# The last image of a two-layer network: bilinear corners gathered from one table per tap instead of one table for all taps

## The chip, the cores and the metric

The kernel runs on one core of a Trainium2 chip. The metric is the device time of one execution in microseconds (us), the median of three runs. The engines are named as in the profile: PE is TensorE (matrix products), DVE is VectorE, ACT is ScalarE, POOL is GpSimd, SP is the engine that issues most DMAs. Each engine works through its own list of instructions in order.

## The reference, cut to what matters

Eight images of 128 channels and 32 by 32 points pass through two layers. The first layer is an attention over columns and rows followed by a long causal convolution (the "spectral" part). The second layer is a deformable convolution with three taps followed by a mixture of eight experts. The change touches only the second layer, and mostly the deformable convolution:

```python
for j in range(K):                                   # K = 3 taps
    y  = h_grid + offset[:, 2 * j]
    xc = w_base + j + offset[:, 2 * j + 1]
    ...
    samp = gather(iy0, ix0) * (1 - wy) * (1 - wx) + gather(iy0, ix0 + 1) * (1 - wy) * wx \
         + gather(iy0 + 1, ix0) * wy * (1 - wx) + gather(iy0 + 1, ix0 + 1) * wy * wx
    samp = samp * mask[:, j][..., None]
    out = out + jnp.einsum('bhwc,oc->bohw', samp, conv_w[:, :, 0, j])
```

For every point and every tap, four corners are read, each is multiplied by a weight, and the twelve products are added up. After that come a normalisation over the channels, a choice of two experts out of eight per point, and the weighted sum of their outputs.

## The kernel before, in words

**Order of the whole.** A first part (up to about 920 us) computes the attention. Then one long loop, `spectral_and_second_layer`, runs over 8 images times 16 filters. Each step issues the spectral products of its filter, and after each small group of them it calls `advance`, which hands out a fixed amount of "time" to two rows of side work. Side work is the second layer of the image before, written as generators that `yield` their own price. The amount handed out is `RATE` (3.2) for images 0 to 6 and `LAST_RATE` (3.6) while the last image, number 7, passes through the spectral part. The program's order on every engine is exactly the order in which these generators issue; nothing reorders it later. When the spectral part of image 7 is done, its own second layer (`layer.image`, which calls `points` and then `sampled` with `alone=True`) is interleaved, step by step, with what is left of image 6's second layer.

**points.** `turn_back` transposes the result back to 128 points x 8 blocks x 128 channels and adds the residual (`tok`, line 1182). `norm_steps` (lines 788 to 795) normalises it. `turn_steps` transposes it. Then, for each of eight blocks of 128 points, one product `p_g` (line 1037) makes the three tap images (3 x 128 values per point) and 27 more values; ScalarE copies the block to `gs` (line 1040). Since the convolution's weights are applied first, a corner is a row of a tap image. `write` (line 1030) stores each tap image four times, shifted by 0, 1, 32 and 33 rows, so that one row of the DRAM table `tab` holds the four corners of a point side by side (4 x 128 numbers, 2 KB). That makes 3 taps x 4 slots x 2 halves = 24 DMAs of 256 KB each. For the last image the slots alternate between SP's queue and ScalarE's queue. `corners` (lines 950 to 981) computes the row numbers `cn_idx` and the weights `w`; between the two, ScalarE makes the exponential of the mask (line 972).

**sampled.** GpSimd issues one indirect DMA (line 1089) per block of points and tap, 24 in all; each fetches 128 rows of 2 KB into one third of a tile `g` (three tiles in rotation). For the last image ScalarE multiplies the corners of taps 0 and 1 by their weights (line 1107, eight instructions per block), VectorE those of tap 2 in one instruction (line 1111), adds all twelve in one reduction (line 1115) and adds `tok` (line 1118). Then follow the normalisation, the gates (lines 1191 to 1228) and, for each block, the experts: two products `p_e` (line 1135), four scalings by ScalarE (line 1142), a product, a reduction and an addition by VectorE (lines 1147, 1152, 1155). After each half of the blocks, `p_out` (lines 1164 and 1167) transposes the result, ScalarE copies it to `ot` (line 1170), and after both halves one DMA of 512 KB writes the image out (line 1172).

**What an instruction waits for.** The waits are placed per DRAM tile: a gather waits until every earlier write to the table it reads has landed. Before the change one table per image parity holds all three taps.

Of the kernel before, what the change touches and what calls it, by code (L numbers as in the profile page):

```python
# [11 lines left out]
F32 = mybir.dt.float32  # L12
I32 = mybir.dt.int32
# [21 lines left out]
RATE = 3.2  # L35
LAST_RATE = 3.6

# [765 lines left out]
class DeformAndExperts:  # L803
# [17 lines left out]
    def setup(self):  # L821
# [30 lines left out]
        for g in range(4):  # L852
# [6 lines left out]
        self.row = cp.tile([P, NT, TAPS], F32, name="row")  # L859
        nc.gpsimd.iota(self.row, pattern=[[0, NT], [self.ROWS, TAPS]], base=33,  # L860
                       channel_multiplier=0, allow_small_or_imprecise_dtypes=True)
# [4 lines left out]
        for n in range(2):  # L866
            tab = dram.tile([TAPS, self.ROWS, 4, C], F32, name=f"tab{n}")
            for tap in range(TAPS):
                for r0 in (0, T):
                    nc.sync.dma_start(  # L870
                        tab[tap, r0 : r0 + 33].rearrange("r s c -> r (s c)"), zero
                    )
                yield
            self.tabs.append(tab)
# [128 lines left out]
    def points(self, b, x2, got, alone, x1):  # L1003
# [21 lines left out]
        def write():  # L1025
            if writes:
                i0, tap, slot, back = writes.pop(0)
                r0 = 33 - back + i0 * P
                queue = nc.scalar if alone and slot % 2 else nc.sync
                queue.dma_start(  # L1030
                    tab[tap, r0 : r0 + 4 * P, slot, :].rearrange("(i p) c -> p i c", p=P),
                    gs[:, i0 : i0 + 4, tap * C : (tap + 1) * C],
                )

        for i in range(NT):
# [5 lines left out]
            if i % 4 == 3:  # L1041
                writes += [
                    (i - 3, tap, slot, back)
                    for tap in range(TAPS) for slot, back in enumerate((0, 1, 32, 33))
                ]
            for _ in range(4 if alone else 2):
                write()
# [20 lines left out]
    def sampled(self, b, got, alone):  # L1068
# [6 lines left out]
        x3 = sb.tile([P, NT, C], F32, tag="x3", name="x3")  # L1075
        rows = self.tabs[b % 2].rearrange("t r s c -> (t r) (s c)")
        points = [(i, tap) for i in range(NT) for tap in range(TAPS)]
        fetched, here, tiles = [], [], []

        def fetch():  # L1080
            if len(fetched) < len(points):
                i, tap = points[len(fetched)]
                if tap == 0:
                    tiles.append(sb.tile([P, TAPS, 4, C], F32, tag="g", name="g", bufs=3))
                    if not alone:
                        here.append(sb.tile([P, TAPS], I32, tag="here", name="here", bufs=3))
                        nc.scalar.copy(here[-1], idx[:, i, :])
                at = idx[:, i, tap : tap + 1] if alone else here[-1][:, tap : tap + 1]
                nc.gpsimd.indirect_dma_start(  # L1089
                    out=tiles[-1][:, tap].rearrange("p k c -> p (k c)"), out_offset=None, in_=rows,  # L1090
                    in_offset=bass.IndirectOffsetOnAxis(ap=at, axis=0),
                )
                fetched.append((i, tap))

        if not alone:
            yield 8.0
        for _ in range(4):
            fetch()
            yield 1.0 if alone else 2.6
        for _ in range(2 if alone else 5):  # L1100
            yield
        for i, tap in points:
# [7 lines left out]
            else:  # L1110
# [7 lines left out]
                nc.vector.tensor_add(x3[:, i, :], x3[:, i, :], tok[:, i, :])  # L1118
            yield 1.7 if alone else 2.6
        tt = sb.tile([P, NT, C], F32, tag="ht", name="tt")  # L1120
# [9 lines left out]
        for i in range(NT):  # L1130
# [26 lines left out]
            if i % 4 == 3:  # L1157
# [4 lines left out]
                for k in range(4):  # L1162
# [6 lines left out]
                    )  # L1169
                nc.scalar.copy(ot[:, half * 512 : half * 512 + 512], po)  # L1170
                yield
        nc.sync.dma_start(self.out[b].rearrange("c h w -> c (h w)"), ot)

# [565 lines left out]
```

## Time and profile before

| what | us |
|---|---|
| median of 3 runs | 2681.59 (2681.54 to 2681.8) |
| the profiled execution, its own time | 2682.64 |
| span of its instructions | 2680.9 |
| PE busy in the span | 2518.2 (94%) |
| last spectral product ends | 2541.7 |
| first table write of image 7 is issued | 2563.64 |
| first gather of image 7 is issued | 2588.68 |
| last corner sum of image 7 ends | 2626.63 |
| copy for the last output DMA ends | 2677.06 |

Times in the table's lower half are counted from the start of the span. The times of the three runs and the profiled one are of separate executions. Of the page, the busy strip is read first: it shows each engine's busy tenths in 40 slices of 67 us. Then the waits and the timeline from 2541 us on are of use, because there the engines do nothing for images other than 7 and a few last steps of image 6.

### The profile page before, as it was taken

The page shows a single profiled execution, that of the slowest core. Times are in us where ns is not written, and L with a number is a line of the kernel's source. Part 1 is how long each engine was busy: PE and PEld are TensorE (multiplying, and loading weights), DVE is VectorE, ACT ScalarE, POOL GpSimd, SP SyncE. Part 2 cuts the span into 40 slices and gives each one's busy share as a digit, 9 for nine tenths or more (in the row PEclk, how much of TensorE's full clock was granted, in tenths as well). Part 3 has the DMA queues.
Part 4 walks back from the last instruction along what each step waited for, and adds up shares of the span by engine and source line. Part 5 has one row for each costly group of instructions (what it writes and reads, how often), then busy time and mean ns, then how long its engine had stood idle before and what let it go on. Part 6 is the DMA issues. An engine that isn't in the chain of part 4 may idle for free. (4 is left out here: it accounts for less than half of the span.)

```text
span 2680.9 us, 47231 instructions
## 1 busy us (share of the span) xinstructions
PE 2518.2 (94%) x18768; PEld 1758.2 (66%) x18768; DVE 1857.6 (69%) x2744; ACT 1074.7 (40%) x2014; POOL 1448.4 (54%) x1535
## 2 busy tenths in 40 slices
PE   6999999999999799999999999999999999999914
PEld 3555555555555478787777778778778778778712
DVE  3788888888888545548748738748748657758646
ACT  4676766766667211123223224214224224224222
POOL 4777777777788455446246236236237327226230
PEclk9999999999999899999999999999999999999956
DMA  1000000000000254475266265256266256246151
GB/s 29 2 17 2 17 17 2 17 2 18 10 18 17 63 172 150 133 209 177 71 203 189 72 196 176 89 179 194 79 185 187 92 161 209 87 138 217 46 171 34
DMA packets 213379, 271.29 MB, mean 101 GB/s; under 512 B 20820, under 2 KB 146964, under 8 KB 213152
## 3 DMA queue, kind: packets, MB, share of 16 engines
q1 hardware_dynamic: 190016, 209.46, 26.1%
q0 software_dynamic: 16800, 55.59, 6.3%
q10 hardware_dynamic: 6336, 3.15, 0.4%
q8 instruction: 150, 2.46, 0.4%
q14 instruction: 77, 0.63, 0.1%
HBM read 200.22 MB, written 67.92 MB: 100 GB/s over the span
## 5 line engine op out<-in xcount | busy, mean ns | idle before, releaser
L623 POOL TENSOR_TENSOR t<-e 128x1024 f32<-128x1024 f32 x256 | 608.2, 2376 | 200.9 <-ACT e L614 200.6
L651 DVE TENSOR_TENSOR e<-e,rb 128x2048 f32<-128x2048 f32 x256 | 570.8, 2278 | 83.6 <-PE rb L644 83.6
L614 ACT ACTIVATE e<-s 128x2048 f32<-128x2048 f32 x256 | 481.1, 1879 | 253.8 <-PE s L609 251.8
L1508 POOL TENSOR_TENSOR part<-us,part 128x256 f32<-128x256 f32 x256 | 189.8, 742 | 695.5 <-ACT part L1507 694.9
L1460 PE MATMUL po<-us,mf 128*128 128x128 f32 (+2 forms) x2048 | 529.0, 381 | 4.4 <-DVE mf L1392 4.4
L1513 DVE TENSOR_TENSOR part<-p_y,part 128x512 f32<-128x512 f32 x256 | 175.5, 686 | 303.7 <-PE p_y L1495 177.0
L1506 ACT COPY us<-p_x 128x256 f32<-128x256 f32 x256 | 95.0, 371 | 724.2 <-PE p_x L1495 721.9
L1460 PEld LDWEIGHTS po<-us,mf 128*128 128x128 f32 x2048 | 309.2, 191 | 36.4 <-DVE mf L1392 4.8
L609 PE MATMUL s<-q,k 32*128 32x256 f32 x4096 | 296.9, 404 | 14.3 <-ACT e L614 13.5
L661 PE MATMUL av<-e,vt 128*32 128x256 f32 x4096 | 288.7, 389 | 4.4 <-DVE e L651 3.1
L1523 DVE TENSOR_TENSOR us<-p_z,part 128x512 f32<-128x512 f32 x256 | 174.9, 683 | 150.7 <-PE p_z L1495 150.6
L609 PEld LDWEIGHTS s<-q,k 32*128 32x128 f32 x4096 | 186.7, 186 | 137.3 <-ACT e L614 116.0
L1495 PEld LDWEIGHTS p_z<-diff,gap 128*128 128x128 f32 x1024 | 192.2, 190 | 128.0 <-issue 87.9
L1495 PE MATMUL p_z<-diff,gap 128*128 128x256 f32 x1024 | 264.8, 380 | 3.5 <-DVE base L906 3.1
L1107 ACT ACTIVATE g<-g,w 128x128 f32<-128x128 f32 x512 | 161.4, 394 | 112.2 <-DMA g<-tab,here 90.8
L1089 POOL DMA_INDIRECT g<-tab,here x168 | 166.0, 988 | 69.7 <-issue 30.5
L661 PEld LDWEIGHTS av<-e,vt 128*32 128x32 f32 x4096 | 101.4, 109 | 141.8 <-issue 84.5
L1115 DVE TENSOR_REDUCE x<-g 128x128 f32<-128x1536 f32 x64 | 180.4, 2818 | 6.8 <-ACT g L1107 1.2
L1250 POOL TENSOR_TENSOR diff<-teto 128x516 f32<-128x516 f32 x127 | 163.9, 1291 | 1.3 <-DMA teto<-in_phi_o 0.5
L637 DVE RECIPROCAL r<-z 128x256 f32<-128x256 f32 x64 | 112.5, 1758 | 70.8 <-PE z L630 70.6
L1495 PE MATMUL p_y<-diff,gap 128*128 128x256 f32 x512 | 152.9, 380 | 0.1
L1495 PE MATMUL p_z<-teto,ht 128*128 128x256 f32 x512 | 133.0, 382 | 0.0
(262 smaller groups left out, 3702.6 us busy)
## 6 DMA issues: line engine op xcount, KB each, us to landing
mf<-mfd SPq DMA_DIRECT2D x112, 512.0 KB
tab<-gs SPq DMA_DIRECT2D x180, 256.0 KB
teto<-in_phi_o SPq DMA_DIRECT2D x127, 256.5 KB
teto<-in_phi_e SPq DMA_DIRECT2D x127, 256.0 KB
mfd<-mf SPq DMA_DIRECT2D x16, 512.0 KB
xc<-in_x SPq DMA_DIRECT2D x8, 512.0 KB
x1d<-xt SPq DMA_DIRECT2D x8, 512.0 KB
m_room<-in_M_plus SPq DMA_DIRECT2D x16, 256.0 KB
```

What stands on the lines that cost most here:

```text
L609: nc.tensor.matmul(s[:, j, c, :], img["k"][rows, hg, 2 * r + c, :], q[rows, qc * QU : (qc + 1) * QU], start=True, stop=True,)
L614: nc.scalar.activation(e.rearrange("p j c q -> p (j c q)"), s.rearrange("p j c q -> p (j c q)"), AF.Exp, scale=float(HD) ** -0.5,)
L623: nc.gpsimd.tensor_add(t, e[:, :, 0, :], e[:, :, 1, :])
L651: nc.vector.tensor_tensor(e, e, un["rb"].unsqueeze(2).to_broadcast([P, NH, 2, QU]), ALU.mult)
L661: nc.tensor.matmul(qrt["av"][32 * j : 32 * j + 32, 0:QU], img["v"][:, 2 * r + c, P * hg + 32 * j : P * hg + 32 * j + 32], un["e", r][:, j, ...
L1089: nc.gpsimd.indirect_dma_start(out=tiles[-1][:, tap].rearrange("p k c -> p (k c)"), out_offset=None, in_=rows, in_offset=bass.IndirectOffs ...
L1115: nc.vector.tensor_reduce(x3[:, i, :], g.rearrange("p t k c -> p c (t k)"), AX.X, ALU.add)
L1460: self.nc.tensor.matmul(out, lhsT, rhs, start=bank not in img["opened"], stop=last, skip_group_check=True)
L1495: nc.tensor.matmul(out, weights, moving, start=start, stop=stop, skip_group_check=True)
L1508: nc.gpsimd.tensor_add(part[:, 0], mine[:, :, 0:P], part[:, 1])
L1513: nc.vector.tensor_tensor(part[:, 2:4], y[:, 0].unsqueeze(1).to_broadcast([C, 2, 2, P]), part[:, 0:2], ALU.add)
L1523: nc.vector.tensor_tensor(result(2, 4), z, part[:, 2:4], ALU.add)
```

## The change

1. `LAST_RATE` goes from 3.6 to 3.75.
2. The table of an image parity is split into three DRAM tiles, one for each tap. The row numbers no longer contain the tap's offset. Images 0 to 6 gather from the three tiles in the same order as before.
3. For the last image, all 24 table writes are issued by SP. The list of pending writes is sorted by tap whenever a half has been added to it. The list is filled half by half and is already in the order of taps, so the order of issue is: first half tap 0, tap 1, tap 2, then second half tap 0, tap 1, tap 2, four writes each.
4. For the last image a new function, `by_taps`, takes the place of the old corner loop: eight gathers of tap 0 first, then taps 1 and 2 of each block in turn. Of each three gathers in that order, the first two are weighted and summed by VectorE, in four chained `scalar_tensor_tensor` instructions each; the third is scaled by ScalarE in four instructions, then reduced and added by VectorE.
5. The output of each image is written in two DMAs of 256 KB, each after its half, instead of one of 512 KB.

```diff
-LAST_RATE = 3.6
+LAST_RATE = 3.75
...
-        nc.gpsimd.iota(self.row, pattern=[[0, NT], [self.ROWS, TAPS]], base=33,
+        nc.gpsimd.iota(self.row, pattern=[[0, NT], [0, TAPS]], base=33,
...
-            tab = dram.tile([TAPS, self.ROWS, 4, C], F32, name=f"tab{n}")
+            tab = []
             for tap in range(TAPS):
+                tab.append(dram.tile([self.ROWS, 4, C], F32, name=f"tab{n}_{tap}"))
...
-                queue = nc.scalar if alone and slot % 2 else nc.sync
-                queue.dma_start(
-                    tab[tap, r0 : r0 + 4 * P, slot, :].rearrange("(i p) c -> p i c", p=P),
+                nc.sync.dma_start(
+                    tab[tap][r0 : r0 + 4 * P, slot, :].rearrange("(i p) c -> p i c", p=P),
...
+                if alone:
+                    writes.sort(key=lambda w: w[1])
...
-        rows = self.tabs[b % 2].rearrange("t r s c -> (t r) (s c)")
-        points = [(i, tap) for i in range(NT) for tap in range(TAPS)]
+        rows = [tab.rearrange("r s c -> r (s c)") for tab in self.tabs[b % 2]]
+        if alone:
+            yield from self.by_taps(idx, w, tok, x3, rows)
+        points = [] if alone else [(i, tap) for i in range(NT) for tap in range(TAPS)]
...
-                nc.scalar.copy(ot[:, half * 512 : half * 512 + 512], po)
+                cols = slice(half * 512, half * 512 + 512)
+                nc.scalar.copy(ot[:, cols], po)
+                nc.sync.dma_start(self.out[b].rearrange("c h w -> c (h w)")[:, cols], ot[:, cols])
                 yield
-        nc.sync.dma_start(self.out[b].rearrange("c h w -> c (h w)"), ot)
+
+    def by_taps(self, idx, w, tok, x3, rows):
+        nc, sb = self.nc, self.sb
+        order = [(i, 0) for i in range(NT)] + [(i, tap) for i in range(NT) for tap in (1, 2)]
+        got = []
+
+        def fetch():
...
+            if n % TAPS == 0:
+                fetch.tile = sb.tile([P, TAPS, 4, C], F32, tag="g", name="g", bufs=3)
+            i, tap = order[n]
+            got.append(fetch.tile[:, n % TAPS])
+            nc.gpsimd.indirect_dma_start(
+                out=got[n].rearrange("p k c -> p (k c)"), out_offset=None, in_=rows[tap],
+                in_offset=bass.IndirectOffsetOnAxis(ap=idx[:, i, tap : tap + 1], axis=0),
+            )
+
+        def scale(n):
+            i, tap = order[n]
+            for k in range(4):
+                nc.scalar.activation(
+                    got[n][:, k, :], got[n][:, k, :], AF.Identity, scale=w[:, i, tap, k : k + 1]
+                )
+
+        for _ in range(5):
+            fetch()
+        for n, (i, tap) in enumerate(order):
+            fetch()
+            if n % TAPS == 0 and n + 2 < len(order):
+                scale(n + 2)
+            so_far = (x3 if tap else tok)[:, i, :]
+            if n % TAPS == 2:
+                both = sb.tile([P, C], F32, tag="both", name="both")
+                nc.vector.tensor_reduce(both, got[n].rearrange("p k c -> p c k"), AX.X, ALU.add)
+                nc.vector.tensor_add(x3[:, i, :], so_far, both)
+            else:
+                for k in range(4):
+                    nc.vector.scalar_tensor_tensor(
+                        x3[:, i, :], got[n][:, k, :], w[:, i, tap, k : k + 1],
+                        x3[:, i, :] if k else so_far, ALU.mult, ALU.add,
+                    )
+            yield 1.3
```

## The prediction, made before the changed kernel ran

> **What bounds the kernel now.** I read the busy strip first, to see which engine holds which part of the span.
>
> ```profile
> PE   6999999999999799999999999999999999999914
> DVE  3788888888888545548748738748748657758646
> DMA  1000000000000254475266265256266256246151
> ```
>
> PE is full from slice 2 to slice 37 (one slice is 67 us): whatever the change adds to PE there is paid in full. Only the last two slices are open, and from 2541.7 us on there is little but image 7. So the change is worth what it does to a tail of 139 us. The tail I read by stretches, with the columns PE, PEld, DVE, ACT and POOL busy, clock, DMA share and GB/s:
>
> ```profile
> 2564.50:2587.00 22.50, 2.88 (x10) 1.73 (x8) 4.29 (x24) 2.14 (x5) 0.00 (x0) 0.58 0.96 280
> 2590.50:2618.50 28.00, 0.00 (x0) 0.00 (x0) 21.75 (x17) 17.46 (x56) 21.60 (x22) 0.50 0.69 198
> ```
>
> In the first the DMA engines are full (0.96 at 280 GB/s) and all else waits: the 24 table writes. In the second POOL issues gathers, DVE sums. The timeline (start, duration, engine, what, idle before it) gives the edges, and the chain of waits the end:
>
> ```profile
> 2563.64 16.72 SPq L1030 DMA_DIRECT2D tab<-gs  x12
> 2588.68 1.05 POOL L1089 DMA_INDIRECT g<-tab,cn_idx  x1 [27.37 <-issue]
> 2592.22 2.62 ACT L1107 ACTIVATE g<-g,w 128x128 f32<-128x128 f32 x8 [11.20 <-DMA g<-tab,cn_idx]
> 2619.00 0.96 POOL L1089 DMA_INDIRECT g<-tab,cn_idx  x1 [0.30 <-issue]
> 2623.58 2.73 DVE x L1115
> ```
>
> The first gather starts 25.04 us after the first write (1.7 us after the last write's data, 2587.0). It lands 3.54 us after its issue; the last corner sum ends at 2626.63, 37.95 us after the first gather began.
>
> **Part by part.**
>
> *LAST_RATE.* The built order shows three products `p_e` of image 6 moved from behind the last spectral product to before it; PE's order changes nowhere else behind it except that eight `p_out` pairs now stand between the two `p_back` groups. A `p_e` takes 0.86 us of PE (two hold it from 2505.27 to 2506.99). PE is full there, so the spectral end moves by +2.6, to 2544.3. What leaves the tail are DVE's three instructions for two blocks, which stand before image 7's statistics:
>
> ```profile
> 2544.73 1.93 DVE L1152 TENSOR_REDUCE both<-ge 128x128 f32<-128x1024 f32 x1
> 2548.28 1.87 DVE L1152 TENSOR_REDUCE both<-ge 128x128 f32<-128x1024 f32 x1
> 2550.40 0.28 DVE L788 BATCH_NORM_STATS2 st<-tok 128x6 f32<-128x128 f32 x1
> ```
>
> Before, statistics begin at 2550.40. After: `p_back` starts at 2542.45 + 2.6 = 2545.05, its four transposes end about 2545.5, the `p_out` group takes 1.8 (2523.38 to 2525.16 earlier), the second `p_back` 0.6, the addition to `tok` 0.69: statistics at 2548.6, **-1.8**. Between 2240 and 2541 PE waited 1.6 us in all, for `tt` at three places; side work that comes 4% faster can make this 0 or 3 (I take 1.6). DVE was 91% busy in image 6's gather stretch (38.26 of 42 us), and 4% more of its side work still fits.
>
> *Writes.* ScalarE no longer issues twelve of them. That had held back its own copies `gs` (to 2570.9) and `cn_m` (2580.80), but both were done before the gathers could start, so it gains nothing. SP alone keeps up: for image 6 it issued 16 writes in 15.49 us, 0.97 each, at the DMA's own pace, 22.7/24 = 0.95 each here; 24 on one queue cost nothing more. The last image's SP has nothing behind the writes but the output.
>
> *First gather.* The sort changes nothing, since the list is filled half by half: tap 0 is complete with the 16th of 24 writes, not the 8th. The first gather waits for 16, so it comes 8 x 0.95 = **-7.6** earlier, 17.5 us after the first write. POOL's row numbers (2576 before) are ready by then. Behind the first gather stand only gathers.
>
> *What is queued after it.* Eight tap-0 gathers take eight POOL pitches of 0.96 + 0.30 = 1.27, some 10 us. The tenth gather (tap 2) waits for the 24th write. When the first gather's data begin to flow (1.5 us after its issue) the DMA has had 3.2 us since the 16th write's end, 0.9 of 2.1 MB; 1.2 MB of writes remain. The writes and the gathers then share the engines. The Trainium skill (DMA: Bandwidth & Descriptors, section "Queues, rings and completion order") says each DMA engine takes turns between queues packet by packet. The table's writes make small packets, the gathers large ones:
>
> ```profile
> q0 software_dynamic: 1920, 6.29, 15.5%
> q10 hardware_dynamic: 6336, 3.15, 7.7%
> ```
>
> That is 3.3 KB against 0.5 KB, so by the rule gathers would run unhindered and the writes starve until POOL stops. The nearest row says otherwise: image 6's first gather, issued at 2417.66 with filter reads ahead of it on SP's queue, was used at 2424.30, 6.64 us after its issue, not 3.54. I take the row, between its two ends: first landing 5 us after issue, and the tenth gather about 2 us late, which DVE's own lag covers nearly (it asks for it at 5 + 9 x 1.48 = 18 us). By the rule alone the result is rival 3.
>
> *Corner sums.* DVE loses, per three gathers, 0.69 + 2.75 + 0.29 with gaps: 3.98 us a block. It gains eight chained pointer-scalar operations, a reduction over 512 values and an addition. No row has 128 elements; the nearest is the same operation with a pointer scalar on 256 and 384:
>
> ```profile
> L1392 DVE SCALAR_TENSOR_TENSOR mf<-both,coef,mf x48: 483/485/836, 932.6 to 1098.4; 128x256 f32<-128x256 f32 x48
> 1097.41 1.87 DVE L1392 SCALAR_TENSOR_TENSOR mf<-both,coef,mf 128x256 f32<-128x256 f32 x3
> ```
>
> 0.485 at 256 and 0.61 at 384 (L1342) make 1 ns an element, so 0.35 at 128; chained ones add 0.03 (1.87 = 0.836 + 2 x 0.515), so 0.38. From below: the form with an immediate scalar, 0.225 at 64, leads to 0.29 + 0.03 = 0.32; from above the unscaled 0.515. I take 0.38, since the pointer is in it. The reduction: 2.75 at 1536 and 1.9 at 1024 lead to 1.06 at 512; with the addition 1.40. Per three gathers 8 x 0.38 + 1.40 = 4.44, against POOL's 3 x 1.27 = 3.8: **DVE becomes the bound**. Eight times 4.44 is 35.5. Less some 1.5 where a chain changes blocks (independent operations start 0.1 earlier), plus 5 to the first landing and 1.3 for the tenth gather (a choice between 0 and rival 3's 4.8): 40.3 us from the first gather to the last sum, against 37.95, **+2.35**. ScalarE's half, 32 scalings instead of 64, hides behind this.
>
> A second rule speaks against the change: the skill (SBUF — State Buffer, section "SBUF: two separate sides") says DVE operations with two SBUF inputs and GpSimd instructions that read SBUF exclude each other for the whole instruction. Such an operation would now run nearly always. The rows:
>
> ```profile
> 2603.05 0.69 DVE L1111 TENSOR_TENSOR g<-g,w 128x512 f32<-128x512 f32 x1 [0.39 <-DMA g<-tab,cn_idx]
> 2603.16 1.42 POOL L1089 DMA_INDIRECT g<-tab,cn_idx  x1 [0.30 <-issue]
> 2611.46 0.69 DVE L1111 TENSOR_TENSOR g<-g,w 128x512 f32<-128x512 f32 x1 [0.60 <-DMA g<-tab,cn_idx]
> ```
>
> A gather begun under L1111 took 1.42, not 0.96: the rest of that operation less 0.13. But L1111 begun 0.09 after the gather of 2611.37 took its usual 0.69. So a gather waits at most 0.35 - 0.13 = 0.22, under 0.1 on average, 2 us in 24 on an engine that is not the bound; VectorE waits for nothing. By the rule VectorE could start only in the 0.3 us between gathers, 64 x 1.27 = 81 us instead of 24: the kernel would be near 2731. I take the row: nothing.
>
> *Output.* Before, the last copy ends at 2677.06 and the 512 KB move from 2678 to 2679.2, 410 GB/s. Half of it takes half: **-0.6**. The first half's DMA stands on SP with nothing behind it but the second.
>
> Everything between the last corner sum and the last copy (50.4 us) keeps its instructions.
>
> **Sum.** -1.8 - 7.6 + 2.35 - 0.6 = -7.65. On the profiled execution's own 2682.6 (span 2680.9) that is 2675.0; the median of the runs shown lies 1.05 below that execution, so the time to compare is 2681.6 - 7.6 = **2674.0**.
>
> **Rivals.**
>
> 1. *Chained operations cheaper* (0.32). Then 8 x (8 x 0.32 + 1.40) = 31.7 after the landing at 5, 36.7 instead of 40.3 (POOL's 23 x 1.27 to the last gather, 3.5 to its landing and 2.7 for its scaling and sum stay below, 35.4): **2670.4**. For it speak the small immediate forms; against it L1392.
> 2. *The split does not bring the start forward*: the first gather is released only with all 24 writes, because DMAs finish together. Then -1.8, -0.4 (landing as before, 3.5 + 34.0 against 37.95), -0.6: **2678.8**, no change by measure. Against it: writes are issued in order and at 0.95 us each, so their ends should be spread alike.
> 3. *Starved writes*: 1.2 MB wait until POOL stops at the tenth gather (11.4 us after the first); 2 us for gathers under way, 4.3 for the 1.2 MB and 1.7 as before from data to issue make 19.4; it lands at 22.9, and 5 x 4.44 = 22.2 of sums follow: 45.1, +7.1, **2678.7**.
> 4. *Slower*: the chain of `x` on DVE. If a chained operation costs the 0.515 that L1392 shows for 256 elements (a cost by instruction rather than by element), three gathers cost 5.52, the stage 49.2 us, +11.3: **2682.9**. It decides from 0.495 on, where 64 of them eat the 9.9 us that the start and the output bring. Against it stands the 0.125 us between 256 and 384 elements.
>
> **Chances.** The likeliest case 0.52 (2670.5 to 2677 by landing and chain), rival 1 0.20, rival 2 0.07, rival 3 0.12, rival 4 0.09. A difference under 0.2% (5.4 us, about what a measurement of this kernel can tell from none) begins at 2676.2. Faster: 0.46 of the first case, 0.20, 0.05 of rival 3 (a milder form) = 0.71; same: 0.06 + 0.07 + 0.07 = 0.20; slower 0.09. The range, 2667.5 to 2680.0, takes in rivals 1 to 3 and leaves out 4, and the edges.
>
> **What would show it.** Right: the first gather 17 to 18 us after the first write; DVE above 90% between landing and last sum, POOL waiting for tiles; chained operations of 0.35; the last DMA 0.6 shorter. Wrong: gathers still starting 25 us after the first write; a gap of several us before the tenth gather; PE waiting more than 2 us before 2541; a DVE operation stretched by every gather.

## The result, and the profile after

| | before | after |
|---|---|---|
| median, us (5 runs each, taken in turn) | 2681.8 (2681.54 to 2688.09) | 2662.22 (2658.17 to 2668.33) |
| profiled execution, its own time | 2682.64 | 2658.17 |
| its span | 2680.9 | 2656.4 |

The ratio after/before is 0.9918, with an interval of 0.99 to 0.9935. The kernel became 0.8% faster, some 20 us. The forecast was 7.6 us, with a range whose lower end is 2667.5: the direction was right, the size was not. The traced execution after is the fastest of its five, 4 us below their median, so the two traces lie 24.5 us apart.

The busy strip of the page after, beside the one of before, shows first where to look, and also how little it tells:

```profile
PE   6999999999999789999999999999999999999924
DVE  3788888888888545549749748658658658658656
DMA  1000000000000154465365266266356357256160
```

PE's row is nearly the same, nines almost throughout: one digit where image 0 begins went from 9 to 8, and the one before the last from 1 to 2, where the prediction had looked. To place the 24.5 us of the traces, cut the span at the copy `x<-po` with which ScalarE closes the spectral part of each image:

| stretch, us | before | after | difference |
|---|---|---|---|
| start to the end of image 0 | 1115.45 | 1112.64 | -2.8 |
| images 1 to 6 | 1227.62 | 1208.45 | **-19.2** |
| image 7 | 198.71 | 204.73 | +6.0 |
| tail, to the end | 139.12 | 130.58 | -8.5 |

The first row is no gain of the change: 2.2 of the 2.8 us are there before the first product of the spectral part (913.97 before, 911.79 after), and in the kernels below that point lies anywhere from 910 to 914 us. So most of the gain came from images 1 to 6, a stretch that ends 200 us before the tail. Here are the rows of these four stretches: engines as before (PE, PEld, DVE, ACT, POOL busy), clock, DMA share, GB/s. First the kernel before:

```profile
1115.45:2343.07 1227.62, 1212.05 (x5582) 949.26 (x5582) 827.13 (x1616) 358.11 (x1122) 556.06 (x799) 1.00 0.50 152
2541.78:2680.90 139.12, 45.26 (x149) 27.22 (x149) 83.48 (x180) 39.90 (x119) 26.79 (x26) 0.63 0.33 98
```

and the kernel after:

```profile
1112.64:2321.09 1208.45, 1203.14 (x5582) 947.11 (x5582) 818.63 (x1616) 357.88 (x1121) 557.89 (x799) 1.00 0.51 154
2525.82:2656.40 130.58, 41.21 (x143) 25.19 (x143) 79.92 (x230) 28.84 (x83) 25.90 (x26) 0.65 0.34 103
```

In the first row of each the matrix products are the same 5582, yet PE was *busy* 8.9 us longer before. The rest of the 19.2 us, 10.3, is waiting. The list of PE's waits in these stretches (who, for whom: us, times, longest) names most of it, before:

```profile
PE p_turn L919 <- DVE tt L795: 8.9, 17, 0.9
```

and after:

```profile
PE p_turn L920 <- DVE tt L795: 0.7, 3, 0.2
```

`p_turn` turns the normalised corner sums of the image before (`tt`) for its gates. Before, PE reached it too early 17 times. The same products also count as busy for longer (busy us, mean ns of one, and the idle time before them, in the same stretches):

```profile
L919 PE MATMUL p_turn<-ident,tt 128*128 128x128 f32 x48 | 10.9, 297 | 9.7 <-DVE tt L795 8.9 <-ACT tc L922 0.7
L920 PE MATMUL p_turn<-ident,tt 128*128 128x128 f32 x48 | 6.9, 276 | 0.7 <-DVE tt L795 0.7
```

A product that stands alone between two waits shows 0.30 us, while eight in a row show 1.04 (both below). So 8.2 us of waits and 4.0 of busy time, 12.2 of the 19.2 us, stand at this one place.

**One image closely.** The table of image 2 (they count from 0) as the example: these are the timelines of GpSimd about its first gather (start, duration, what, in brackets the idle time before it and what ended it). Before:

```profile
1589.22 0.73 POOL L1508 TENSOR_TENSOR part<-us,part 128x256 f32<-128x256 f32 x1 [5.13 <-ACT part L1507]
1595.32 1.05 POOL L1089 DMA_INDIRECT g<-tab,here  x1 [5.37 <-DMA teto<-in_phi_o]
1596.39 1.29 POOL L1250 TENSOR_TENSOR diff<-teto 128x516 f32<-128x516 f32 x1
```

After, the same place:

```profile
1582.60 0.79 POOL L1557 TENSOR_TENSOR part<-us,part 128x256 f32<-128x256 f32 x1 [5.13 <-ACT part L1556]
1583.74 1.05 POOL L1091 DMA_INDIRECT g<-tab,here  x1 [0.36 <-DMA tab<-gs]
```

Before, GpSimd stood 5.37 us in front of the gather, with all that its list holds behind it; after, 0.36. The same goes for each of images 0 to 6: 3.92, 4.37, 5.37, 4.27, 5.35, 4.62 and 4.41 us before; 0.20 to 0.65 after. (The releaser before is put down to a filter read that shared the queue with the table's writes. That the writes are what it waits for, the experiments show.) Some 80 us later PE reaches that image's `p_turn`. Before:

```profile
1676.81 0.60 PE L919 MATMUL p_turn<-ident,tt 128*128 128x128 f32 x4
1677.87 0.30 PE L919 MATMUL p_turn<-ident,tt 128*128 128x128 f32 x1 [0.46 <-DVE tt L795]
1678.46 0.33 PE L919 MATMUL p_turn<-ident,tt 128*128 128x128 f32 x1 [0.30 <-DVE tt L795]
1679.65 0.58 PE L919 MATMUL p_turn<-ident,tt 128*128 128x128 f32 x2 [0.85 <-DVE tt L795]
1680.07 1.56 PE L1495 MATMUL p_z<-diff,gap 128*128 128x256 f32 x4
1681.42 1.91 PE L1495 MATMUL p_z<-teto,ht 128*128 128x256 f32 x4
```

After:

```profile
1669.10 1.04 PE L920 MATMUL p_turn<-ident,tt 128*128 128x128 f32 x8
1669.98 1.03 PE L1544 MATMUL p_z<-diff,gap 128*128 128x256 f32 x4
```

The waits of before add to 1.61 us. The two groups of four `p_z` that follow take 1.56 and 1.91 us; after, the first takes 1.03. The stretches of before at this place say why (length, PE busy, clock, DMA share, GB/s):

```profile
1677.03:1680.44 3.41, 1.80 (x10) 1.00 0.91 284
1680.44:1683.85 3.41, 3.41 (x10) 0.50 0.07 22
```

After 3.41 us in which PE was busy for 1.80 the clock was at a half for the next 3.41 us, in which PE was busy throughout: 1.7 us of work lost. That loss hides in the busy time and in the strip's nines. But it is the smaller part of it. In images 1 to 6 it happened twice, here and from 2093.45 us on, 3.4 us in all. The six stretches of before are longer by 1.7, 2.1, 5.2, 2.3, 5.1 and 2.8 us, and the two large ones are these. The waits for `tt`, the busy time of `p_turn` and the half clock together are 15.6 of the 19.2 us; the rest was not followed.

**The tail**, for which the prediction had been worked out, came much as worked out. The edges after:

```profile
2543.08 21.53 SPq L1030 DMA_DIRECT2D tab<-gs  x24
2560.85 1.05 POOL L1192 DMA_INDIRECT g<-tab,cn_idx  x1 [19.94 <-DMA tab<-gs]
2565.44 0.35 DVE L1217 SCALAR_TENSOR_TENSOR x<-g,w,tok 128x128 f32<-128x128 f32 x1 [13.89 <-DMA g<-tab,cn_idx]
2598.69 2.94 DVE L1217 SCALAR_TENSOR_TENSOR x<-g,w,x 128x128 f32<-128x128 f32 x8
2601.55 1.01 DVE L1213 TENSOR_REDUCE both<-g 128x128 f32<-128x512 f32 x1
```

The first gather comes 17.8 us after the first write, its data 4.6 us after that, and the last sum ends at 2602.88, 42.0 us after the first gather.

### The profile page after: what moved, and what is told of

Same layout as the page of the kernel before. It is cut to its first block, busy times and chain, and to the rows that moved or that the text cites. A ratio compares the mean times of both kernels' runs of the same rounds, so it can differ in the third digit from the quotient of the medians.

```text
span 2656.4 us, 47332 instructions
## 1 busy us (share of the span) xinstructions
PE 2500.7 (94%) x18768; PEld 1750.2 (66%) x18768; DVE 1852.6 (70%) x2800; ACT 1064.2 (40%) x1982; POOL 1449.2 (55%) x1535
## 5 line engine op out<-in xcount | busy, mean ns | idle before, releaser
L623 POOL TENSOR_TENSOR t<-e 128x1024 f32<-128x1024 f32 x256 | 608.2, 2376 | 198.9 <-ACT e L614 198.7
L1109 ACT ACTIVATE g<-g,w 128x128 f32<-128x128 f32 x448 | 140.1, 393 | 74.2 <-DMA g<-tab,here 73.2
L1117 DVE TENSOR_REDUCE x<-g 128x128 f32<-128x1536 f32 x56 | 158.7, 2834 | 5.0
L1544 PE MATMUL p_x<-teto,ht 128*128 128x256 f32 x512 | 131.4, 379 | 0.0
```

The source lines that it names most:

```text
L623: nc.gpsimd.tensor_add(t, e[:, :, 0, :], e[:, :, 1, :])
L1544: nc.tensor.matmul(out, weights, moving, start=start, stop=stop, skip_group_check=True)
```

## The experiments

Each kernel is measured beside the kernel before on the same chip; the ratio is to that. The last four columns are of one profiled execution each: images 1 to 6, image 7 and tail as in the table above, and the idle time of GpSimd in front of the first gathers of images 0 to 6.

| kernel | ratio, interval | images 1-6 | image 7 | tail | idle |
|---|---|---|---|---|---|
| before | 1 | 1227.6 | 198.7 | 139.1 | 3.9 to 5.4 |
| after | 0.9918 [0.99, 0.9935] | 1208.5 | 204.7 | 130.6 | 0.2 to 0.7 |
| e1_split_only | 0.9937 [0.9916, 0.9959] | 1210.4 | 201.3 | 137.3 | 0.3 to 0.7 |
| e2_whole_tables | 0.998 [0.9972, 0.9988] | 1227.9 | 208.8 | 133.0 | 3.3 to 5.2 |
| e3_rate36 | 0.9931 [0.9907, 0.9955] | 1210.1 | 201.3 | 135.4 | |
| e4_old_corners | 0.9912 [0.9888, 0.9936] | 1210.9 | 205.7 | 133.3 | |
| e5_tap_order | **0.9888** [0.9868, 0.9907] | 1209.2 | 204.4 | 126.4 | |
| e6_late_gather | 0.9956 [0.9939, 0.9973] | 1214.3 | 200.7 | 143.6 | 0.4 to 0.9 |
| e7_pairs | 0.9889 [0.9869, 0.9908] | 1211.2 | 204.1 | 127.5 | |
| e8_pairs_rate39 | 0.9903 [0.9884, 0.9922] | 1211.7 | 208.6 | 126.3 | |
| e9_issue_only | 1.0024 [1.0014, 1.0034] | 1231.3 | 201.3 | 138.1 | 0.4 to 1.0 |
| e10_use_only | 0.9973 [0.9954, 0.9993] | 1216.5 | 197.6 | 142.2 | 4.1 to 5.2 |
| e11_tap_order_rate36 | 0.9904 [0.9888, 0.9921] | 1208.9 | 202.7 | 131.8 | |

### Which part of the change made it: e1 and e2

e1 is the kernel before with nothing but the split tables (and row numbers without the tap's offset), for all eight images. e2 is the changed kernel with one table per image parity again for images 0 to 6, and three for the last image alone.

```diff
--- e2, against after
...
-        for n in range(2):
+        for n in range(3):
             tab = []
+            if n < 2:
+                self.whole.append(dram.tile([TAPS, self.ROWS, 4, C], F32, name=f"tab{n}"))
             for tap in range(TAPS):
-                tab.append(dram.tile([self.ROWS, 4, C], F32, name=f"tab{n}_{tap}"))
+                if n < 2:
+                    tab.append(self.whole[n][tap])
+                else:
+                    tab.append(dram.tile([self.ROWS, 4, C], F32, name=f"tab{n}_{tap}"))
...
-        tab = self.tabs[b % 2]
+        tab = self.tabs[2 if alone else b % 2]
...
+        if alone:
+            rows = [tab.rearrange("r s c -> r (s c)") for tab in self.tabs[2]]
+        else:
+            rows = TAPS * [self.whole[b % 2].rearrange("t r s c -> (t r) (s c)")]
```

> The kernel before with nothing but the table split by tap, for all eight images; order of writes and gathers, queues, corner sums, rate and output as before. Theory A (the unforeseen gain comes from images 0 to 6, where GpSimd stood 4 to 5.4 us at each image's first gather until all 24 writes had landed, with other images' work queued behind it): the stretch from the end of image 0's spectral part to that of image 6 falls from 1227.6 us to about 1208, the time to about 2662. Theory B (the gain lies in the last image, or is a difference between executions): the stretch stays near 1227, the time at 2680 to 2682.

> The changed kernel, but images 0 to 6 use one table for all taps again, and only the last image has three. Theory A: the stretch of images 1 to 6 is back at about 1227 us, GpSimd's first gathers wait 4 to 5 us again, and the time is near 2662 + 19 = 2681, less what the tail keeps: about 2676 to 2680. Theory B: 2662, with a stretch near 1208.

With the split alone, images 1 to 6 take 1210.4 us, and the kernel is 0.63% faster. With everything but the split of images 0 to 6 they take 1227.9, as before, and all the rest of the change is worth 0.2% (its interval, 0.12 to 0.28%, is 3.2 to 7.5 us). The wait at the first gather is back with the whole table:

```profile
1590.16 1.05 POOL L1103 DMA_INDIRECT g<-tab,here  x1 [5.16 <-DMA teto<-in_phi_o]
```

So that is a wait for all 24 writes, and the split of the first seven images' tables is some three quarters of the gain (e1 splits the last image's table as well; its tail is 1.8 us shorter than before, in one execution each). The trace of e2 divides its small gain otherwise than one would expect: the tail is 6.1 us shorter, image 7's stretch 10.0 longer, and the span up to the end of image 0 is 7.5 shorter (3.7 of it before the spectral part begins), where the change does no more than set up its tables.

### The terms of the last image: e3 and e4

```diff
--- e3, against after
-LAST_RATE = 3.75
+LAST_RATE = 3.6
--- e4, against after
-        if alone:
-            yield from self.by_taps(idx, w, tok, x3, rows)
-        points = [] if alone else [(i, tap) for i in range(NT) for tap in range(TAPS)]
+        points = [(i, tap) for i in range(NT) for tap in range(TAPS)]
...
```

> The changed kernel with LAST_RATE back at 3.6. As I predicted the rate (worth 1.8 us by itself): about 2664. By the trace of the changed kernel (in image 7's stretch PE waits 2.3 us for a filter difference and 1.6 for the normalised tile, about 6 us at one step, which the kernel before does not have): this goes away, three expert products move back into the tail, and the time is about 2656 to 2659.

> The changed kernel with the old corner loop for the last image (block by block, ScalarE two thirds, one reduction over twelve), the split tables, SP's writes and the rest kept. If the new corner loop is worth its early start: the third gather of the first block now waits for all 24 writes (25 us after the first write), so the last corner sum comes 25 + 38 - 2.5 = 60.5 us after the first write against 59.8 measured: no more than 1 us slower, about 2662. If the early start was the gain of the tail (7.6 us less what the chain costs): about 2667 or more.

By the profiles of after and e3 the higher rate takes 4.8 us off the tail and puts 3.4 on image 7's stretch, 1.4 net; the medians (2662.2 and 2664.2) were taken on different chips, and the intervals overlap. Of the 3.4 us, 2.7 are work: image 7's stretch has 44 instructions for `p_e` in after (21.0 us) and 38 in e3 (18.3), as predicted. The rest is the sum of waits that come and go. The largest new one is at a place where GpSimd's Newton steps now stand before a filter difference that PE needs:

```profile
2457.82 1.27 POOL L1299 TENSOR_TENSOR diff<-teto 128x516 f32<-128x516 f32 x1
2457.89 3.34 DVE L795 TENSOR_SCALAR tt<-x,mv,rs_y 128x128 f32<-128x128 f32 x4 [2.97 <-POOL rs_y L778]
2459.14 0.70 PE L1544 MATMUL p_y<-diff,gap 128*128 128x256 f32 x2 [2.34 <-POOL diff L1299]
```

In e3 PE does not wait for `diff` there, but 2.5 us for `tt` (1.6 in after) and 1.1 us for `us` (none in after). e4 puts the old order of corners (block by block) on the split tables. Its first gather comes as early, but the second waits 2.22 us and the third 3.52 us for the tables of taps 1 and 2, and from the first write to the last sum it takes 61.6 us, against 59.8 with the new function and 63.0 before. Its ratio cannot be told from that of after: what `by_taps` adds to the split is some 2 us.

### Writes in the order of taps: e5, e7, e8 and e11

The list of writes is filled half by half, so tap 0 is complete with the 16th write. e5 holds the writes of the last image back until a half is complete, and then writes by tap.

```diff
--- e5, against after
             for _ in range(4 if alone else 2):
-                write()
+                if not alone or i in (3, 7):
+                    write()
```

> The changed kernel with the last image's 24 writes really in the order of taps: tap 0 of both halves first, then tap 1, then tap 2. If the start of the gathers is what the tail hangs on: the first gather comes 7.6 us earlier after the first write, about 10.2 us instead of 17.8, and the last corner sum up to 7 us earlier (53 us after the first write instead of 59.8). If the writes that then remain (16 of 24) share the DMA engines with the gathers, gathers of taps 1 and 2 wait for their tables, and the last sum comes no more than 2 to 4 us earlier (56 to 58 us).

It has the lowest ratio of all, 2655.63 us (2652.49 to 2657.24), though its interval overlaps that of after. The first gather comes 11.0 us after the first write, and the last sum after 55.6 instead of 59.8. GpSimd's timeline shows what then holds:

```profile
2562.99 0.98 POOL L1193 DMA_INDIRECT g<-tab,cn_idx  x1 [0.30 <-issue]
2571.24 1.00 POOL L1193 DMA_INDIRECT g<-tab,cn_idx  x1 [7.28 <-DVE both L1214]
```

After nine gathers the tenth, the first of tap 2, waits 7.28 us. VectorE's `both`, which is named, had ended at 2562.82; the last writes, issued until 2566.2, had not landed. The stretch between says that the DMA engines were the limit (0.97 at 318 GB/s):

```profile
2552.60:2571.20 18.60, 0.00 (x0) 0.00 (x0) 11.63 (x30) 3.83 (x12) 8.88 (x9) 0.50 0.97 318
```

So the tenth gather is late, as rival 3 had it, but not by starved writes. These are the queues from 2556 to 2569 us, while the data of the first nine gathers flow (packets, MB, share of 16 engines), the writes first:

```profile
q1 hardware_dynamic: 4981, 2.47, 63.9%
q0 software_dynamic: 720, 2.36, 45.1%
```

The two move the same amount side by side, though a gather's packets are larger (3.3 KB on average, against 0.5). The writes are late because 16 of them, not 8, are still to come; and the gathers fared no better by it, for their first data took 4.97 us. Of the 7 us by which the first gather came earlier, 4 were kept.

e7 takes e5 and divides the work otherwise: VectorE alone for tap 0, ScalarE's scalings for taps 1 and 2, one reduction over eight corners for each block.

```diff
--- e7, against e5
+            if tap == 0:
                 for k in range(4):
                     nc.vector.scalar_tensor_tensor(
...
+            else:
+                for k in range(4):
+                    nc.scalar.activation(
...
+            if tap == 2:
+                both = sb.tile([P, C], F32, tag="both", name="both")
+                nc.vector.tensor_reduce(
+                    both, g[:, 0:2].rearrange("p t k c -> p c (t k)"), AX.X, ALU.add
+                )
```

> As e5_tap_order, and the sums dealt out anew: tap 0 by VectorE alone (8 chains of four), taps 1 and 2 of a block scaled by ScalarE and added in one reduction over eight corners. VectorE then needs 8 x 1.51 + 8 x 2.25 = 30 us instead of 35.5, less than GpSimd's 24 x 1.27 + 3.5. If VectorE's chain is the bound of the stage: 4 to 5 us less from first gather to last sum than in e5_tap_order. If the landing of the gathers is: less than 2 us.

VectorE is busy for 28.3 us in that stage instead of 31.9 after and some 32 in e5, and nothing is won: the tenth gather again waits 7.02 us for the writes. VectorE's chain is no longer the bound once the gathers start early. Two rates beside that complete it:

```diff
--- e8, against e7
-LAST_RATE = 3.75
+LAST_RATE = 3.9
--- e11, against e5
-LAST_RATE = 3.75
+LAST_RATE = 3.6
```

> As e7_pairs with LAST_RATE 3.9. By the predicted accounting (work moved from the tail to the full PE) within 2 us of e7_pairs. If the wait of PE for a late filter difference in image 7's stretch (2.3 us, with about 6 us lost at that step) is a matter of where the side work falls, it may vanish or double: that stretch, 204.7 us in the changed kernel, moves by several us either way.

> The kernel e5_tap_order (2655.6, the changed kernel with the writes of the last image held until a half is complete for every tap) with LAST_RATE back at 3.6. From the pair after and e3_rate36 (image 7's stretch 3.4 shorter, the tail 4.8 longer) the sum is 1.4 us longer: 2657, ratio about 0.9894. If the rate's gain in the tail came from the writes waiting for image 6's sums, the same holds here; if it came from the slower start of gathers, which e5 has already removed, the rate is worth nothing or costs: 2653 to 2655.

3.9 takes another 1.2 us from the tail and puts 4.4 on image 7's stretch, whose trace has 10.24 us at half clock (from 2462.31), 5.1 us lost, that e7 does not have. 3.6 gives 1.7 us back in image 7 and takes 5.4 in the tail. Both intervals overlap that of 3.75: nothing is left to win with this number.

### Why a late gather costs PE anything: e6, e9 and e10

The first theory was: GpSimd, standing in front of a gather, holds up the filter differences, partial sums and Newton steps in its list, on which PE and VectorE wait. e6 is the kernel before with all from the first gather on placed 6 units later in the program.

```diff
--- e6, against before
-            yield 8.0
+            yield 14.0
```

> The kernel before (one table) with the first gather of images 0 to 6 placed 6 units of side work later in the program (about 5 us). If the cost before was that GpSimd stood in front of its queue for the writes: it no longer stands there, the filter differences, sums and Newton steps behind it are on time, the stretch of images 1 to 6 falls from 1227.6 to 1212 or less and the time to about 2668. If the cost was that the gathers themselves come late (so that the normalisation behind them falls on busier steps): the stretch stays at 1227 or grows, since they now come 1 us later still.

Images 1 to 6 fall to 1214.3 us: the program's order alone takes 13 us out of this stretch, with whole tables. Not all of that is gain: the stretch has 4 instructions for `p_e` and 16 for `p_out` less, 3.6 us of PE's work that now comes later, and the tail is 4.5 us longer; the kernel gains 0.44%, 12 us. And e6 moves two things, the issue of the gathers and the use of their data. e9 and e10 part them. In e9 the order on PE and VectorE is that of before, instruction for instruction; on GpSimd the first gathers go behind the Newton steps.

```diff
--- e9, against before
-            yield 8.0
+            yield 13.0
...
-        for _ in range(2 if alone else 5):
+        for _ in range(2 if alone else 0):
--- e10, against before
-        for _ in range(2 if alone else 5):
+        for _ in range(2 if alone else 11):
```

> The kernel before, with only the place of the first four gathers of images 0 to 6 in the program changed: they are issued 5 units later, and the sums that use them stand where they stood, so the order of PE and VectorE is the same instruction for instruction; on GpSimd the first gathers now stand behind the Newton steps and the filter differences that they used to hold up. Theory queue (what cost 19 us is the work that stood behind a GpSimd waiting for the table writes): GpSimd waits under 1 us at each first gather, the images 1 to 6 take about 1211 us instead of 1227.6, and the time is 0.993 of before. Rival lateness (what cost is that the gathered rows come too late for VectorE's sums): the rows come no earlier than before, so the stretch stays at 1226 to 1230 and the ratio is 0.999 to 1.002.

> The kernel before, with the first gathers of images 0 to 6 where they are and only their use (the sums and all behind them) 6 units later in the program. GpSimd still waits 4 to 5.4 us at each first gather, and the Newton steps behind it are still late. Theory queue: VectorE is still 3 us late from those Newton steps on, so about 1.1 us of each image stays lost (a loss where the next image's turned columns wait), and what was lost at the later normalisation (some 2 to 4 us an image) may be hidden by the later place: stretch 1217 to 1228, ratio 0.995 to 1.0. Rival lateness: all of the loss goes, stretch 1209 to 1213, ratio 0.9925 to 0.994.

The time that the theory forecast for e9 did not come. GpSimd no longer stands in front of a gather (it waits 2.84 us for VectorE instead, ahead of the Newton steps),

```profile
1605.19 1.05 POOL L1089 DMA_INDIRECT g<-tab,here  x1 [0.94 <-DMA teto<-in_phi_o]
```

and the kernel is 0.24% *slower*; the wait of PE is unchanged:

```profile
PE p_turn L919 <- DVE tt L795: 9.3, 17, 0.9
```

But e9 is not a clean test of it. At image 2 the Newton steps come 2.5 us earlier after the image's `x` copy, and VectorE's `xc`, which needs them, starts 1.7 us earlier. Then the gain is gone; the first line is before, the others are e9:

```profile
1608.30 2.54 DVE L795 TENSOR_SCALAR xc<-x,mv,rs_y 128x128 f32<-128x128 f32 x6
1609.23 4.23 DVE L795 TENSOR_SCALAR xc<-x,mv,rs_y 128x128 f32<-128x128 f32 x6
1610.67 1.28 POOL L1250 TENSOR_TENSOR diff<-teto 128x516 f32<-128x516 f32 x1
1614.40 1.32 POOL L1262 TENSOR_TENSOR gap<-xc 128x512 f32<-128x512 f32 x1 [1.02 <-DVE xc L795]
```

Six pieces of `xc` take 1.7 us longer. One of them, beside GpSimd's `diff`, takes 2.10 us; a piece with GpSimd at a gather takes 0.34. It is the same at each of images 0 to 5 in e9 (at every second one the tile is called `ht`). GpSimd's `gap` waits for `xc`, the fifth gather stands behind `gap`, and it comes when it came before. So e9 shows that this order does not help; whether early Newton steps would help without that collision stays open.

In e10 GpSimd stands as long as before (5.03 us for the same image), but `p_turn` comes later in PE's list, and its wait is gone from the list. The ratio, 0.9973, is inside what the first theory gave for it, the stretch, 1216.5, at the edge; the rival had both lower. So the numbers of e9 speak against the first theory and those of e10 for it, and the waits say more. The only new one in e10 is

```profile
PE p_back L1180 <- DVE x L1537: 8.0, 5, 1.6
```

five times 1.6 us where the image is turned back, which e6 has as well: the later use pushed other work into that place. (It looks like just the difference to the 1208.5 of after, but the stretch of e10 also has three half-clock stretches, 5.1 us lost, and the same 3.6 us of PE's work less as in e6.)

What does fit is seen by following image 2 through four kernels, each time counted from the image's own `x` copy (worked out from the timelines, us):

| | before | after | e9 | e10 |
|---|---|---|---|---|
| first gather issued | 78.3 | 73.3 | 85.5 | 82.2 |
| fifth gather | 96.2 | 93.1 | 96.2 | 101.5 |
| last Newton step of the next column turn | 86.9 | 83.4 | 84.4 | 90.8 |
| last gather | 132.6 | 129.3 | 132.6 | 139.1 |
| last corner sum starts its last addition | 145.5 | 140.7 | 145.5 | 151.6 |
| last Newton step for `tt` | 155.9 | 151.1 | 155.8 | 162.9 |
| `p_turn` starts | 159.8 | 158.7 | 159.8 | 168.1 |
| PE's waits inside it | 1.6 | 0 | 1.6 | 0 |

GpSimd is the pacemaker from the first gather to the last: after the first few, gathers follow its other work with 0.2 to 0.3 us between. What it loses ahead of that row it does not make up before, 3.3 us at the last gather, 4.8 at the last sum and at the Newton steps. `p_turn` stands in PE's list where before it comes 3.9 us behind the last Newton step, and VectorE needs 6.7 us to make `tt` (156.1 to 162.8). After and e10 need 4.9: pieces of `tt` take 0.3 us by themselves and 0.7 to 1.3 beside GpSimd's `diff` and `part`, and before six of the eight stand beside these, after three. In e9 the Newton steps of the column turn came 2.5 us earlier, and the rest stayed to a tenth as before. So most of the cost sits at one place, `tt` against `p_turn` (1.1 of the 5.2 us by which the stretch from this `x` copy to the next is longer are lost before it, about a wait of 0.45 us for VectorE's `us`). Two changes took that wait away: rows that come sooner (the split), and a later place for the use (e6, e10). How much of the 19.2 us each link of this chain costs is read from the traces; no run took the links one by one.

The half clock is the one link that e9 parts from the rest, by chance. At image 2 PE waits there as before, 1.57 us against 1.61, but the clock stays full; the last two lines are stretches as above:

```profile
1680.47 0.30 PE L919 MATMUL p_turn<-ident,tt 128*128 128x128 f32 x1 [0.41 <-DVE tt L795]
1681.07 0.33 PE L919 MATMUL p_turn<-ident,tt 128*128 128x128 f32 x1 [0.30 <-DVE tt L795]
1682.25 0.59 PE L919 MATMUL p_turn<-ident,tt 128*128 128x128 f32 x2 [0.86 <-DVE tt L795]
1682.68 1.03 PE L1495 MATMUL p_z<-diff,gap 128*128 128x256 f32 x4
1677.21:1680.62 3.41, 3.00 (x16) 1.00 0.79 219
1680.62:1684.04 3.42, 2.26 (x11) 1.00 0.75 245
```

From this `x` copy to the next e9 takes 205.76 us, before 207.49: the 1.7 us that the half clock costs. With the same list of waits it came twice in images 1 to 6 before and once in e9. In each trace the half-clock stretches start a whole number of 3.413 us apart (1680.44 and 2093.45: 121 of them), as if on a fixed grid. Before, one step of this grid held 1.80 us of PE's work; in e9 the same waits are divided over two, with 3.00 and 2.26. So whether such a wait costs the clock depends on where it falls.

## Why the prediction was wrong, and where it was right

**The step that failed** is in the first paragraph on the bound: "PE is full from slice 2 to slice 37 ... So the change is worth what it does to a tail of 139 us." From it followed that the split tables of images 0 to 6 were never costed. Two readings would have shown it. PE's list of waits was read from 2240 to 2541 us alone. It shows 1.6 us for `tt` there (and 2.3 for `p_back`, so "1.6 us in all" was read too low); from 1115 to 2343 it shows 8.9 for `tt` in 17 parts. The runs showed in place of the zero: 19.2 us in the traces, 17 by e1's ratio. And GpSimd's timeline at any first gather shows 4 to 5 us in front of a table that the diff was about to split. A strip of nines says that an engine is busy nine tenths of the time; of 1227 us a tenth is 123, and busy time at half clock is counted as busy.

The terms of the sum, as predicted and measured:

| term | predicted | measured |
|---|---|---|
| images 0 to 6, split tables | 0 | -19.2 in the trace; e1's ratio, -17 in all |
| `LAST_RATE`, net | -1.8 | -1.4 (e3 against after, profiles) |
| its cost at PE's end, within that | +2.6 | +3.4 (e3 against after), 2.7 of it the moved products; +6.0 for image 7 after against before |
| first gather after the first write | 17.5 | 17.8 |
| first data after that | 5 | 4.6 |
| first gather to last sum | 40.3 | 42.0 |
| output in halves | -0.6 | -0.6 (3.2 us from the last copy to the end, 3.8 before) |

- *Writes and first gather.* The mechanism and the size were right, and rival 2 (released only with all writes) is out: 17.8 us, not 25. So is rival 3 (starved writes): the tenth gather was not late, 0.30 us behind the ninth. Statistics came earlier as worked out: from the last `x` copy to the first write it takes 17.3 us instead of 21.9 (-4.6, where -1.8 and -2.6 had been predicted).
- *Corner sums.* 0.35 for the pointer-scalar operation, 0.38 in a chain, 1.02 for the reduction, as taken; rivals 1 and 4 are out by the size of the row. A block takes 4.2 us in the steady part (4.44 less what the change of blocks saves). VectorE is not above 90% busy, but 31.90 of 37.6 us, 85%: it waits 1.55 us for the second and third landing, and about 2 us between 2586 and 2591 for its own operations, which the profile does not explain. The 1.3 us predicted for the tenth gather were not used. The sum of this came out 1.7 us too small.
- *The port.* No operation of VectorE is stretched beside a gather, and gathers keep 0.95 to 1.06 us. Taking the row and not the rule was right. What did get longer beside GpSimd is VectorE's `xc` and `tt`, next to GpSimd's arithmetic and not its gathers (e9: 2.10 us for 0.34); the prediction did not look at these.
- *Image 7's stretch.* PE waits were to be 0 to 3 us by the higher rate. They became 2.3 for `diff` and 1.6 for `tt`, and the stretch grew by 6.0, not 2.6; e1 and e3, at the old rate, show 2.6 of the 6.0 as well, so that part is not the rate's (image 7's stretch has image 6's second layer in it; in e1's trace PE waits 2.4 us for `tt` and 1.1 for `us` there, before it does not; why was not sought out); 3.4 come with the rate.

By the ratios the predicted terms by themselves were near: e2, which leaves out the split of the first seven images, is 5.4 us faster than before, and after is some 5 us faster than e1 (with intervals that overlap), where 7.65 had been worked out. Part of that nearness is luck. In the traces the tail and image 7's stretch together give 2.5 us (after against before), and e2's gain stands before the end of image 0. With 17 us for the first term the sum would have been 25 us, some 5 too many against the medians.

## What to carry to other kernels

An object that several readers wait for as a whole (here a DRAM table) has a price wherever it is used, so list every wait on it over the whole span before restricting a sum to the part that a change is named for. In a stretch that one engine fills, read its waits and its clock over that whole stretch; an engine that paces others and stands still once, even off the critical path, can be late at each later meeting point. Here earlier data and a later place for their use both took the wait away. And when work is moved, see what it then stands beside: in e9 what the new order gained was lost again in one instruction.

## What the runs showed of the hardware

- The clock halved after 3.41 us in which PE was busy for 1.80, with no wait longer than 0.85 us, and came back after 3.41 us. The Trainium skill (TensorE: Matmul & The Clock Gate, section on the HAM clock gate) says that the clock halves after an idle window of about 3.4 us. The length agrees; the condition was milder than idle. No bound follows from these runs: before, 1.95 us of work brought the half clock as well (from 2093.45) and in e9 2.26 did not, but in e2 a step of the grid with 1.59 us (from 2473.99) was followed by the full clock.
- VectorE's operations get longer beside GpSimd's arithmetic: one piece of `xc` took 2.10 us beside `diff` and 0.34 otherwise (e9, at six images), pieces of `tt` 0.7 to 1.3 and 0.3 (before and after). Beside the issue of a gather in the tail of after they did not.
- With writes and gathers together, the DMA engines moved 318 GB/s (e5) against 280 with the writes alone; the first gather's data came 4.6 us (8 writes left) and 4.97 us (16 left) after its issue, 3.54 with no write left. While both moved, each had half of the bytes (e5: 2.47 and 2.36 MB).
- One kernel's runs spread by up to 16 us (before, beside e9: 2672.99 to 2688.95). In the traces up to 3.7 us are in place when the spectral part begins (910.2 to 914.0).
